# The start of a fused attention and feed-forward kernel: queries computed tile by tile, x added on TensorE, conversions and transfers in another order

## The chip, the cores and the metric

The kernel runs on one core of a Trainium2 chip. The metric is device time in microseconds. The core has TensorE (the rows PE and, for its weight loads, PEld), VectorE (DVE), ScalarE (ACT), GpSimd (POOL) and SyncE (SP). Each works through its own list of instructions in order, and they wait for one another by semaphores. Transfers are issued by SP, POOL or ACT.

## The reference

Input: 4096 tokens of 256 features in fp32. One block of linear attention (no softmax), a layer norm, a gated feed-forward net of width 1024 and a second layer norm:

```python
Q, K, V = x @ wq.T, x @ wk.T, x @ wv.T            # 64 columns each
energy  = K.T @ V                                 # 64 x 64, over all tokens
x = layernorm(x + (Q @ energy * sqrt(3/64)) @ wo.T)
h = silu(x @ w1.T * s1) * (x @ w2.T * s2)         # 1024 wide
h = gelu(h @ h1.T * hs1)
h = gelu(h @ h2.T * hs2)
x = layernorm(x + h @ w3.T * s3)
```

The energy needs the keys and values of all tokens before the first token's attention can be finished. Nothing behind it can start before it.

## The kernel before

The tokens are cut into eight tiles of 512 (`T`), the tiles are numbered 0 to 7, and a tile has four blocks of 128 tokens (index `s`). TensorE's outputs go to eight PSUM banks of 128x512 fp32; `aux` is banks 6 and 7, `ring` the three pairs (4, 5), (0, 1) and (2, 3). Most products keep fp32 accuracy by cutting one operand in two: ACT casts it to the rounded format `fp32r` (`hi`), DVE subtracts to get the rest (`lo`), and TensorE multiplies both parts with weights that are exact in that format. Products of plain fp32 operands run as two matmul records each.

The kernel has a start, in which keys, values, queries and the energy are made, and then four passes over pairs of tiles: gates (16 steps, eight column groups for each of two tiles), two square layers of 1024x1024 done with sums and differences of quarter matrices, and the last product with its norm. The start overlaps with the first pass, and the change lies there. The order of every engine's instructions is the order of the Python code (a manual schedule); no planner moves them.

In order, the start does this:

- Transfers. SP issues the first tile `xt[0]` in two halves with the weights `wkv` between them (L440, L442), then tiles 1 to 7 (L444), with `wq` behind tile 3, then `raw_blocks(0, 0)`, a transfer of a square layer's raw weights (L471), the tokens `x` of tile 0 and the scales. POOL issues `wo`, and `w1` and `w2` in halves (L530, L534); each waits for an earlier transfer by `after`. The loads of `x` of tile 1 on SP wait until the first half of `w1` has landed; `raw_blocks(0, 1)`, `s3` and `raw_blocks(0, 2)` stand behind them on SP.
- Six warm-up products (L549), then `keys_values` of tiles 0 to 3 (L574), each evacuated by an ACT copy of the whole bank (L580).
- `halves` of tiles 4 and 5 (L624 `hi` on ACT, L625 `lo` on DVE), all emitted behind the copy of tile 3, then `with_queries` of tiles 4 to 7 (L593): keys, values and queries in one product, evacuated in two groups `g` (L598, L599 on ACT, L600 on DVE). `halves(t + 1)` goes ahead of `with_queries(t)`.
- `two_queries(0)` (L645): queries of tiles 0 and 1, one in the upper, one in the lower 64 partitions of a bank; `stack` (L653 on ACT, L655 on DVE) puts `hi` into one half of the partitions of `stk[t]` and `lo` into the other, so that one product with the stacked operand does both. Tiles 4 to 7 get theirs by a transposition on TensorE (`turn_queries`, L608) and an ACT copy (`put_queries`, L612).
- `energy` (L633, eight tiles into 64 columns of bank 6), scaled by ACT (`es`, L679), times `wo` (L682, bank 7), cut into `m2hi` (ACT, L683) and `m2lo` (DVE, L684).
- `attention_out(0)` (L140): four 256-column products for each of two groups, hi and lo, into banks 6 and 7. DVE adds them onto `x` (L163), takes statistics (L150, L152), adds the epsilon (L87); POOL raises to the power -1/2 (L88); DVE norms (L172). TensorE transposes the result (L203), ACT and DVE cut it (L211, L212): these are the operands of the gates.
- Between these stand products that fill TensorE: `two_queries(2)` (tiles 2 and 3) in two parts, `turn_queries` of tiles 4 to 7.
- The first three gate steps for the first 256 tokens (`first_products`, L728; ring pairs 0, 1, 2), with the transposition of the second 256 tokens behind step 1; then the same three steps for the second half (L718); then `attention_out(1)`, and `gate` for steps 0 to 2 (ACT's silu L737 and DVE's product L738 free the banks). From step 3 on all steps are 512 columns wide.
- `early[0]` to `early[3]` are sums of raw weight blocks on DVE (L310) with a store by POOL (L494); the first two need `raw_blocks(0, 0)`, the others `raw_blocks(0, 1)`.

Of the kernel before, what the change touches and what calls it, by code (L numbers as in the profile page):

```python
# [44 lines left out]
def block_kernel(ctx: ExitStack, tc: tile.TileContext, a: dict, out: bass.AP):  # L45
# [85 lines left out]

    def attention_out(t):
        ps = []
        for g in range(NS // 2):
            po = aux[g].rearrange("p (j e) -> p j e", j=2)

            for i, m in enumerate((m2hi, m2lo)):
                for j in range(2):
                    q = stk[t][:, (2 * g + j) * P : (2 * g + j + 1) * P]
                    nc.tensor.matmul(  # L140
                        po[:, j, :], q, m, start=(i == 0 and j == 0), stop=(i == 1 and j == 1),
                        skip_group_check=True,
                    )
            ps.append(po)
        return ps
# [7 lines left out]

    def attend_norm(t, x, ps, pool):

        mv = p2.tile([P, NS, 2], F32, tag="mv1", name=f"mv1_{t}")
        y = pool.tile([P, NS, E], F32, tag=f"x2_{t // 2 % 2}", name=f"x2_{t}", bufs=2)
        r = {}
        x2[t] = y

        def add(g, j=slice(0, 2)):
            u = x[:, 2 * g : 2 * g + 2, :][:, j, :]
            nc.vector.tensor_tensor(u, u, ps[g][:, j, :], ALU.add)  # L163

        def stats(g):
            norm_stats([x[:, 2 * g + j, :] for j in range(2)], mv, 2 * g)

        def root(g):
            r[g] = rstd_of(p2, mv[:, 2 * g : 2 * g + 2, :], "a", 2)

        def norm(s, engine=nc.vector):
            engine.tensor_scalar(  # L172
                y[:, s, :], x[:, s, :], mv[:, s, 0:1],
                r[s // 2][:, s % 2 : s % 2 + 1], ALU.subtract, ALU.mult,
            )

        def norm_on_act(minus):

            for s in range(NS):
                nc.scalar.activation(  # L180
                    y[:, s, :], x[:, s, :], AF.Identity, bias=minus[:, s : s + 1], scale=1.0
                )
                nc.scalar.activation(
                    y[:, s, :], y[:, s, :], AF.Identity, scale=r[s // 2][:, s % 2 : s % 2 + 1]
                )

        def minus_mean():
            m = p2.tile([P, NS], F32, tag="mm", name=f"mm{t}")
            nc.vector.tensor_scalar(m, mv[:, :, 0], -1.0, None, ALU.mult)
            return m  # L190

        norm.on_act = norm_on_act, minus_mean
        return add, stats, root, norm

    def turn_on_pe(t, slot):
# [4 lines left out]
        def turn(s0, s1):  # L200
            for k in range(KE):
                for s in range(s0, s1):
                    nc.tensor.transpose(  # L203
# [234 lines left out]
    last = {}  # L438
    for k in range(KE):
        nc.sync.dma_start(out=xt[0][:, k, :], in_=a["xt"][0][:, k, :])  # L440
        if k == 0:
            nc.sync.dma_start(out=wkv, in_=a["wkv"])  # L442
    for t in range(1, NT):
# [72 lines left out]
    for name, dst in (("s1", s1), ("s2", s2), ("hs1", hs1), ("hs2", hs2)):  # L516
        nc.sync.dma_start(out=dst, in_=a[name])


    def after(d, t):  # L520
# [14 lines left out]
    xs[1] = load_x(1, lambda d: after(d, "w1"))  # L535
    raw_blocks(0, 1, raws[1])
    nc.sync.dma_start(out=s3, in_=a["s3"].partition_broadcast(P))
    after(raw_blocks(0, 2, raws[2])[0], "w2")


    turn_of_acc = [7]

# [10 lines left out]

    pe = aux[0][:, :D]
    xh, xl, kv, pq = {}, {}, {}, {}
# [26 lines left out]
    def with_queries(t):  # L582
# [4 lines left out]
        for g in range(2):  # L587
            ps = acc()[:, : 2 * V].rearrange("p (s c) -> p s c", s=2)
            for j in range(2):
# [11 lines left out]
                q[:, c, 1, :], ps[:, :, 2 * D :], q[:, c, 0, :].bitcast(F32), ALU.subtract  # L601
            )

    def turn_queries(t):
        ps = acc()
        for s in range(NS):
# [11 lines left out]
    def halves(t):  # L618

        xh[t], xl[t] = places[t - WHOLE]  # L620
        n = 2 if t == WHOLE else 1
        for h in range(n):
# [14 lines left out]

    def two_queries(t, steps=range(4)):

        if t not in pq:  # L640
            pq[t] = pq[t + 1] = acc()
        for i in steps:
            c, k = slice((i // 2) * T // 2, (i // 2 + 1) * T // 2), i % 2
            for j in range(2):
                nc.tensor.matmul(  # L645
                    pq[t][j * D : (j + 1) * D, c], wq1[:, k, :], xt[t + j][:, k, c],
                    start=(k == 0), stop=(k == KE - 1),
                )

    def stack(t):  # L650

        up, down = (slice(0, D), slice(D, P))[:: 1 - 2 * (t % 2)]
        nc.scalar.copy(stk[t][up], pq[t][up])  # L653
        yield
        nc.vector.tensor_tensor(stk[t][down], pq[t][up], stk[t][up].bitcast(F32), ALU.subtract)  # L655
        yield

    early = [*sums(0, 0, raws[0]), *sums(0, 1, raws[1])]
    for t in range(NT):
        if t < WHOLE:  # L660
            keys_values(t)
            continue
        if t == WHOLE:
            halves(t)
            halves(t + 1)
        elif t + 1 < NT:
            halves(t + 1)
        with_queries(t)
    two_queries(0)
    early[0]()  # L670
    for _ in stack(0):
        pass
    stack1 = stack(1)
    next(stack1)

    for t in range(NT):
        energy(t)
    two_queries(2, [0])
    nc.scalar.mul(es, pe.unsqueeze(1).to_broadcast([P, 2, D]), CSCALE)  # L679
    early[1]()  # L680
    pm = aux[1][:, :E]
    nc.tensor.matmul(pm, es.rearrange("e c d -> e (c d)"), wo, start=True, stop=True)  # L682
    nc.scalar.copy(m2hi, pm)  # L683
    nc.vector.tensor_tensor(m2lo, pm, m2hi.bitcast(F32), ALU.subtract)  # L684
    next(stack1)
    turn_queries(WHOLE)
    po = attention_out(0)
    put_queries(WHOLE)
    for t in range(WHOLE + 1, NT):
        turn_queries(t)  # L690
        put_queries(t)
    two_queries(2, range(1, 4))
    add, stats, root, norm = attend_norm(0, xs[0], po, p2)
    for j in range(2):
        add(0, j)
    stats(0)
# [4 lines left out]
    norm(1)  # L701
    stats(1)
    root(1)
    slot = next_slot()
    turn, split = turn_on_pe(0, slot)
    turn(0, 2)
    split(0, 2)
    norm(2)
    norm(3)
    for t in (2, 3):  # L710
        for _ in stack(t):
            pass

# [28 lines left out]

    for o in range(3):
        first_products([*zip(ring[o], (w1, w2))], o, slot, slice(0, T // 2))
        if o == 1:
            turn(2, 4)
            split(2, 4)
            early[2]()
            early[3]()
    for o in range(3):  # L750
        for ps, w in zip(ring[o], (w1, w2)):
# [6 lines left out]
    nc.gpsimd.dma_start(out=w3, in_=a["w3"])  # L758
    gate(0, xb)
    gate(1, xb)  # L760
    add(0)
    gate(2, xb)
    add(1)
    for g in range(2):
        stats(g)
        root(g)
    turn, split = turn_on_pe(1, slot)
    for i in range(3, 2 * KH):
        for ps, w in zip(ring[i % 3], (w1, w2)):
            gate_products(ps, w, i % KH, slot, i // KH)  # L770
        gate(i, xb)
        if i == 3:
            for s in range(NS):
# [613 lines left out]
```

## Time and profile before

| | |
|---|---|
| Median of 3 runs | 641.39 us (639.77 to 643.33) |
| Profiled execution | 639.2 us, span 637.3 us |
| TensorE busy | 623.9 us, 98% |
| DVE busy | 487.8 us, 77% |
| ACT busy | 378.8 us, 59% |
| First matmul of keys and values | 3.80 us from the span's start |
| First matmul of tile 1 | 7.60 us |
| First `with_queries` | 14.42 us |
| First product of queries alone | 23.52 us |
| First gate product (L728) | 34.44 us |
| First 512-column gate product (step 3) | 43.10 us |
| First product of a square layer (L298) | 69.92 us |

All times inside an execution are counted from the start of the span. A line of the waits reads: engine and line that waited, what ended the wait, microseconds in total, number of waits, the longest. A matmul's row in the trace includes its way through the array, so that rows overlap; its cost to the next one is the distance from start to start.

### The profile page before, as it was taken

To read this page: it belongs to the slowest core of one execution; us is meant where nothing else is said; L and a number is where in the kernel's file an instruction comes from. 1 tells how busy PE (TensorE), PEld (TensorE's weight loads), DVE (VectorE), ACT (ScalarE), POOL (GpSimd) and SP (SyncE) were. 2 spreads that over 40 slices of the span, in tenths; PEclk is the share of its full clock that TensorE was granted. 3 is DMA by queue.
4 is the path that set the end of the run, shared out by engine and by line. 5 is a ranking of instruction groups with operands and counts; after the bars stand their busy time and mean duration, and the time that the engine had idled before them with its cause. 6 is when DMAs were issued, how large, how long until landed. Compare 5 with 4: busy or idle time off the path is not lost.

```text
span 637.3 us, 9037 instructions
## 1 busy us (share of the span) xinstructions
PE 623.9 (98%) x3173; PEld 527.1 (83%) x3173; DVE 487.8 (77%) x764; ACT 378.8 (59%) x542; POOL 218.0 (34%) x280
## 2 busy tenths in 40 slices
PE   7999999999999999999999999999999999999995
PEld 6878888888898888888898888888898888888895
DVE  1799984898678788888667798798676886697456
ACT  3545462659855374656755458757764557765574
POOL 1233113204865408405545604612653700000043
PEclk9999999999999999999999999999999999999998
DMA  8999769987652168647751135645861035543201
GB/s 322 289 361 301 239 212 361 271 278 227 168 162 70 49 220 267 218 145 217 227 152 34 66 117 187 227 163 174 227 164 32 35 125 176 168 161 132 100 1 68
DMA packets 59408, 113.31 MB, mean 178 GB/s; under 512 B 19776, under 2 KB 34112, under 8 KB 59232
## 3 DMA queue, kind: packets, MB, share of 16 engines
q1 hardware_dynamic: 41168, 74.28, 35.1%
q0 software_dynamic: 18192, 38.41, 19.8%
q8 instruction: 26, 0.43, 0.3%
q14 instruction: 22, 0.18, 0.1%
HBM read 96.94 MB, written 18.87 MB: 182 GB/s over the span
## 4 chain that ended last, share of the span: by engine, by line
PE 95%; DVE 2%; DMA 1%; ACT 1%; issue 1%; POOL 0%; SPq 0%; POOLq 0%; DVEq 0%
PE bank L298 64%; PE bank L718 18%; PE bank L873 9%; PE bank L140 1%; PE bank L574 1%; PE bank L593 1%; DMA f<-in_xt 1%; PE bank L645 0%; DVE stk L655 0%; DVE lo L625 0%; DVE bn L150 0%; PE bank L633 0%; ACT hi L624 0%; POOL ra L88 0%; PE bank L728 0%
## 5 line engine op out<-in xcount | busy, mean ns | idle before, releaser
L298 PE MATMUL bank<-hi,ws 128*128 128x512 f32 x896 | 348.7, 389 | 0.0
L298 PE MATMUL bank<-lo,ws 128*128 128x512 f32 x896 | 348.6, 389 | 0.0
L253 DVE TENSOR_TENSOR lo<-f,hi 128x1024 fp32r<-128x1024 f32 x142 | 168.3, 1224 | 59.6 <-ACT hi L252 59.0
L298 PEld LDWEIGHTS bank<-hi,ws 128*128 128x128 f32 x896 | 168.2, 188 | 34.9
L298 PEld LDWEIGHTS bank<-lo,ws 128*128 128x128 f32 x896 | 168.2, 188 | 34.9
L252 ACT CAST hi<-f 128x1024 fp32r<-128x1024 f32 x142 | 142.7, 1051 | 48.6 <-PE bank L298 25.1
L348 ACT ACTIVATE f<-f,hs 128x512 f32<-128x512 f32 x96 | 62.6, 715 | 68.7 <-DVE f L310 68.7
L718 PE MATMUL bank<-hi,w 128*128 128x512 f32 (+1 forms) x256 | 98.4, 386 | 0.0
L718 PE MATMUL bank<-lo,w 128*128 128x512 f32 (+1 forms) x256 | 98.1, 385 | 0.0
L737 ACT ACTIVATE f<-bank,s 128x512 f32<-128x512 f32 x64 | 44.0, 689 | 68.2 <-PE bank L718 63.7
L310 DVE TENSOR_TENSOR f<-f,f 128x1024 f32<-128x1024 f32 x64 | 76.5, 1221 | 4.5 <-ACT f L348 3.8
L310 DVE TENSOR_TENSOR f<-f,bank 128x512 f32<-128x512 f32 x96 | 61.4, 681 | 15.3 <-ACT f L403 11.3
L738 DVE SCALAR_TENSOR_TENSOR f<-bank,s,f 128x512 f32<-128x512 f32 x64 | 47.6, 748 | 25.1 <-PE bank L718 24.0
L873 PE MATMUL bank<-w,lo 128*128 128x256 f32 x240 | 57.9, 283 | 0.0
L873 PE MATMUL bank<-w,hi 128*128 128x256 f32 x240 | 57.9, 283 | 0.0
L237 POOL DMA_DIRECT2D xT<-x x96 | 52.2, 551 | 13.1 <-DMA stage<-in_h 5.5
L718 PEld LDWEIGHTS bank<-hi,w 128*128 128x128 f32 x256 | 48.1, 188 | 9.8 <-DVE d L882 0.4
L718 PEld LDWEIGHTS bank<-lo,w 128*128 128x128 f32 x256 | 48.1, 188 | 9.3
L835 POOL DMA_DIRECT2D stage<-in_h x16 | 9.2, 575 | 126.8 <-DVE stage L861 99.7
L873 PEld LDWEIGHTS bank<-w,lo 128*128 128x128 f32 x240 | 46.1, 192 | 0.2
L873 PEld LDWEIGHTS bank<-w,hi 128*128 128x128 f32 x240 | 46.0, 192 | 0.2
L403 ACT COPY f<-bank 128x512 f32<-128x512 f32 x32 | 18.6, 589 | 28.6 <-PE bank L298 28.5
(161 smaller groups left out, 545.2 us busy)
## 6 DMA issues: line engine op xcount, KB each, us to landing
ws<-sw SPq DMA_DIRECT2D x100, 512.0 KB, 3.5
sw<-so POOLq DMA_DIRECT2D x16, 512.0 KB, 4.9
stage<-in_h POOLq DMA_DIRECT2D x16, 512.0 KB, 5.0
ws<-in_h POOLq DMA_DIRECT2D x12, 512.0 KB, 6.4
sw<-in_h SPq DMA_DIRECT2D x12, 512.0 KB, 5.9
x<-in_x SPq DMA_DIRECT2D x16, 256.0 KB, 6.0
f<-in_xt SPq DMA_DIRECT2D x7, 512.0 KB, 7.3
f<-in_h SPq DMA_DIRECT2D x6, 512.0 KB, 9.8
```

The lines of the kernel that those rows point to most:

```text
L237: moves.popleft()()
L252: nc.scalar.copy(hi[:, c, :], src[:, c, :])
L253: nc.vector.tensor_tensor(lo[:, c, :], src[:, c, :], hi[:, c, :].bitcast(F32), ALU.subtract)
L298: nc.tensor.matmul(ps[2 * h + o], w[:, k, o * P : (o + 1) * P], part[i][:, k, :], start=start and k == 0 and i == 0, stop=k == HK - 1 and ...
L310: engine.tensor_tensor(dst, u, v, op)
L348: nc.scalar.activation(dst, src, AF.Gelu, scale=sc[:, o : o + 1])
L403: nc.scalar.copy(bb[:, o], al[o])
L718: nc.tensor.matmul(ps[:, c], w[:, k, o * P : (o + 1) * P], part[:, 2 * j + k, c], start=(k == 0 and i == 0), stop=(k == KE - 1 and i == 1),)
L737: nc.scalar.activation(g, pa, AF.Silu, scale=s1[:, o : o + 1])
L738: nc.vector.scalar_tensor_tensor(g, pb, s2[:, o : o + 1], g, ALU.mult, ALU.mult)
L835: nc.gpsimd.dma_start(out=st[:, :n], in_=src.rearrange("p k o -> p (k o)")[:, c : c + n])
L873: nc.tensor.matmul(ps[:, :E], part[q][:, k, s * P : (s + 1) * P], w3[:, k0 + k, :], start=i % 2 == 0 and k == 0 and q == 0, stop=i % 2 == ...
```

## The change

The change rearranges the start:

- Transfers. `wkv` and the second half of `xt[0]` are issued by ACT, the first half by SP. `raw_blocks(0, 1)` goes ahead of the loads of `x` of tile 1 on SP.
- Conversions. `halves(4)` is emitted between the keys and values of tiles 2 and 3, `halves(5)` behind tile 3; `halves(6)` and `halves(7)` go between and behind the two groups of `with_queries(4)`. Tile 7 is cut in two parts, as tile 4 is.
- Queries of tiles 0 to 3. `queries(t, ps)` computes one tile at a time, with its two halves of 256 tokens in the upper and lower 64 partitions, into half a bank. `stack(t)` becomes two casts and two subtractions of 64x256. Tile 0's queries stand ahead of the energy, tile 1's behind attention, tiles 2 and 3 between the first two gate steps, together with `turn_queries` of tiles 6 and 7.
- `x` of the first two blocks of tile 0 is added by TensorE: a product with the identity (`with_x`) begins the accumulation in bank 0, and the attention of group 0 goes on in that bank. Statistics and norms of these blocks read the bank; the DVE additions are gone. The second group is added by DVE as before.
- Banks: the energy and its product with `wo` go into bank 4, and fixed banks replace the turn of `acc()` for queries and turns.
- Gates: the first two steps, not three, are done in halves; step 2 is done in 512 columns, and the additions and statistics of tile 1 are interleaved accordingly. Transpositions run by block instead of by feature half. `early[2]` and `early[3]` change places with stacks and norms.

```diff
     def attend_norm(t, x, ps, pool, summed=()):
+        def total(s):
+            return ps[s // 2][:, s % 2, :] if s // 2 in summed else x[:, s, :]
...
+    nc.scalar.dma_start(out=wkv, in_=a["wkv"])
+    for k, queue in enumerate((nc.sync, nc.scalar)):
+        queue.dma_start(out=xt[0][:, k, :], in_=a["xt"][0][:, k, :])
...
+    raw_blocks(0, 1, raws[1])
...
-    turn_of_acc = [7]
+    turn_of_acc = [3]
...
-        n = 2 if t == WHOLE else 1
+        n = 2 if t in (WHOLE, NT - 1) else 1
...
+    def queries(t, ps):
+        pq[t] = ps
+        for k in range(KE):
+            for j in range(2):
+                nc.tensor.matmul(
+                    ps[j * D : (j + 1) * D], wq1[:, k, :],
+                    xt[t][:, k, j * T // 2 : (j + 1) * T // 2],
+                    start=(k == 0), stop=(k == KE - 1),
+                )
     def stack(t):
+        sides = [slice(j * D, (j + 1) * D) for j in range(2)]
+        halves = [stk[t][:, j * T // 2 : (j + 1) * T // 2] for j in range(2)]
+        for s, h in zip(sides, halves):
+            nc.scalar.copy(h[s], pq[t][s])
+        for s, o, h in zip(sides, sides[::-1], halves):
+            nc.vector.tensor_tensor(h[o], pq[t][s], h[s].bitcast(F32), ALU.subtract)
...
+    for t in range(3):
+        keys_values(t)
+    halves(4)
+    keys_values(3)
+    halves(5)
+    for t in range(WHOLE, NT):
+        for g, _ in enumerate(with_queries(t)):
+            if t == WHOLE:
+                halves(6 + g)
+    queries(0, bank[1][:, :E])
     early[0]()
+    stack(0)
     for t in range(NT):
         energy(t)
     nc.scalar.mul(es, pe.unsqueeze(1).to_broadcast([P, 2, D]), CSCALE)
     early[1]()
+    with_x(0)
     nc.tensor.matmul(pm, es.rearrange("e c d -> e (c d)"), wo, start=True, stop=True)
     nc.scalar.copy(m2hi, pm)
     nc.vector.tensor_tensor(m2lo, pm, m2hi.bitcast(F32), ALU.subtract)
+    with_x(1)
+    po = attention_out(0, (bank[0], aux[1]), (0,))
+    for t, ps in ((4, bank[5]), (5, bank[2])):
+        turn_queries(t, ps)
         put_queries(t)
+    queries(1, bank[1][:, E:])
+    add, stats, root, norm = attend_norm(0, xs[0], po, p2, (0,))
     stats(0)
     root(0)
     for j in range(2):
         add(1, j)
     norm(0)
     norm(1)
     turn(0, 2)
+    stack(1)
     split(0, 2)
+    stats(1)
+    root(1)
+    early[2]()
     norm(2)
     norm(3)
...
+    first_products([*zip(ring[0], (w1, w2))], 0, slot, slice(0, T // 2))
+    turn_queries(6, bank[3])
+    put_queries(6)
+    queries(2, bank[2][:, :E])
+    queries(3, bank[2][:, E:])
+    turn_queries(7, bank[3])
+    put_queries(7)
+    turn(2, 4)
+    split(2, 4)
+    first_products([*zip(ring[1], (w1, w2))], 1, slot, slice(0, T // 2))
+    early[3]()
+    stack(2)
+    stack(3)
+    for o in range(2):
         for ps, w in zip(ring[o], (w1, w2)):
             gate_products(ps, w, o, slot, 0, slice(T // 2, T))
...
     gate(0, xb)
+    add(0)
     gate(1, xb)
     add(1)
+    for i in range(2, 2 * KH):
...
+        if i == 2:
+            for g in range(2):
+                stats(g)
+                root(g)
```

## The prediction

> **What bounds the kernel now.** First the page: busy shares, and the chain that ended last.
>
> ```profile
> PE 623.9 (98%) x3173; PEld 527.1 (83%) x3173; DVE 487.8 (77%) x764; ACT 378.8 (59%) x542; POOL 218.0 (34%) x280
> ...
> PE   7999999999999999999999999999999999999995
> ...
> PE 95%; DVE 2%; DMA 1%; ACT 1%; issue 1%; POOL 0%; SPq 0%; POOLq 0%; DVEq 0%
> ```
>
> TensorE is the bound everywhere except in the first slices, and the diff touches only those. So the question is how many microseconds in which TensorE does nothing are left there. Second, TensorE's waits in the first 90 us:
>
> ```profile
> PE bank L574 <- DMA f<-in_xt: 1.3, 1, 1.3
> PE bank L593 <- ACT hi L624: 1.2, 1, 1.2
> PE bank L728 <- DVE stk L655: 0.9, 1, 0.9
> PE bank L593 <- DVE lo L625: 0.9, 2, 0.6
> PE bank L728 <- ACT hi L211: 0.2, 1, 0.2
> PE bank L203 <- DVE x L172: 0.2, 1, 0.2
> ```
>
> These add up to 4.7 us, but a matmul's modelled tail counts as busy, so I also compare stretches with pure work. Third, the busy time by stretch (columns: stretch, length, busy of PE, PEld, DVE, ACT, POOL, then the granted clock, DMA share, GB/s):
>
> ```profile
> 3.65:7.60 3.95, 2.54 (x17) 2.38 (x17) 0.43 (x2) 0.99 (x2) 0.00 (x0) 1.00 0.98 314
> 7.60:13.22 5.62, 5.62 (x48) 5.43 (x48) 0.53 (x3) 1.17 (x2) 0.00 (x0) 1.00 1.02 403
> 13.22:23.50 10.28, 8.21 (x65) 7.52 (x64) 6.54 (x12) 8.15 (x20) 4.17 (x6) 1.00 0.89 286
> 23.50:34.44 10.94, 10.46 (x127) 7.58 (x127) 8.83 (x24) 4.93 (x12) 2.27 (x3) 1.00 1.05 347
> 34.44:43.10 8.66, 7.72 (x60) 7.45 (x61) 7.72 (x17) 3.99 (x8) 2.70 (x4) 1.00 0.95 369
> 43.10:69.92 26.82, 26.82 (x131) 22.38 (x130) 26.15 (x47) 13.63 (x19) 9.77 (x15) 1.00 1.04 302
> 18.70:21.00 2.30, 1.69 (x16) 1.52 (x14) 1.93 (x4) 1.97 (x6) 1.99 (x3) 1.00 0.35 73
> ```
>
> From start-to-start times in the timeline, one record costs 0.117 us (keys and values, transposes), 0.112 (`with_queries`, and queries at 64 columns of the array), 0.029 (energy), 0.12 (256-column gate or attention) and 0.228 (512-column gate). Work and bubbles (time minus work) are then: tile 0 with the wait for tile 1, 1.9 and 2.1; tiles 4 to 7, 7.2 and 3.1; from the queries to the first gate product, 9.2 and 1.7; from there to gate step 3 at 43.10, 7.2 and 1.5. That is 8.4 us of bubbles, and none behind 43.10. DVE is busy 26.15 of the 26.82 us there: by the timeline it frees the banks for gate steps 13 and 14 only 0.1 us before TensorE wants them.
>
> **The change, part by part.** The clock row is 1.00 throughout, so times carry over.
>
> *First transfers.* Each issue on SP takes 0.38 to 0.43 us plus 0.05. `wkv` and the second half of tile 0 go to ACT's queue; that puts tile 1's issue at about 1.27 instead of 2.21. It landed 5.3 us after issue, at 7.55, bound by the bytes ahead of it; later tiles land every 1.3 to 1.45 us. With the same delay tile 1 lands at 6.6; with no effect, at 7.55. The second half of tile 0 landed at 5.04; ending it means 5.9 at the earliest, the lower bound for tile 1. I take 6.5, nearest to the issue rows. ACT loses 0.9 us to its two issues ahead of its table load, hidden before `wkv` lands. Tiles 1 to 3 then run from 6.5 to 12.1 (5.62 us). Bubble 2.1 becomes 1.0.
>
> *Conversions of tiles 4 to 7.* Before, `halves(4)` stood behind tile 3's copy on ACT, so TensorE waited from 13.22 to 14.42, and again at 19.79 for `lo` of tile 6. Now `halves(4)` goes ahead of that copy: ACT is free at 10.95 (tile 2's copy, 0.59), tile 4 has landed by then (11.7 minus 0.9), the casts take 0.62 each and `lo` 0.69 each, done by 12.8, so tile 4 starts without a gap. What is late next is tile 5: ACT does tile 3's copy to 12.75, `hi` (1.05) to 13.8, DVE's `lo` (1.23) to 15.05, while TensorE wants it at 14.1: a stall of 1.0. Behind it `halves(6)` and `halves(7)` (in two parts) follow tile 4's evacuations on ACT (0.37 + 0.27 each) and come in time, within 0.2. So 8.4 us instead of 10.28: queries start at 20.5 instead of 23.5.
>
> *From the queries to the first gate product.* Moved behind the first gate product: the queries of tiles 2 and 3 (1.8) and the turns of tiles 6 and 7 (0.94), 2.75 in all; those of tile 1 (0.9) go behind attention. Added: `x` by an identity, two full-width fp32 products. Nearest by shape is 0.234 per 256 columns and record (twice the 128-column row), 0.94 in all; the 64-column queries' 0.112 gives 0.45 as low end, the `wo` product's 0.35 mean gives 1.4 as high end. They stand in front of and behind the `wo` product, where TensorE waits for `es` and for `m2hi` and `m2lo`, so of 0.94 only 0.1 shows. If that cover goes, all of it does. Removed from DVE: two bank additions (0.75), and `stack(1)` (0.69) ahead of them. `bn_stats` now reads the bank: 0.37 each, as the SBUF row, since additions that read banks (0.375) cost no more; bounds 0.30 and 0.50.
>
> With 0 at the start of the queries: queries to 0.9, energy to 2.76, `es` to 3.15, `wo` product 3.25 to 3.95, `m2hi` to 4.35; DVE does the two sums and `stack(0)` (now two halves, 0.75) until 4.6, so `m2lo` ends at 5.0; attention's first group at 5.4; statistics 0.97 and the epsilon row 0.17 to 6.55; POOL's power 0.73 with 0.15 of handover to 7.43; two norms to 8.2; transposes to 8.6; `hi` 0.37; first gate product at 9.0. Fillers (turns of 4 and 5, one tile's queries, attention's second group) end at 7.55. Before, this took 10.94; work is 7.4, so the bubble is 1.6. The first gate product comes at 29.5 instead of 34.44. Its banks are free by then (bank 4 by `m2lo` at 5.0, bank 5 by tile 4's evacuation at 6.9); bank 0, which the norms now hold, is free at 8.2 and wanted at 13.4. The stores of the sums take 0.77 of POOL each; those of the first two are issued by 5.4, ahead of the power at 6.7, and `early[2]` stores behind the second power. Transposing by token block instead of by half lets the first two go before the second norm ends; 0.2 at most, counted.
>
> The Trainium skill (VectorE: DVE Perf Modes, The perf-mode tier table) says that fp32 `tensor_scalar` runs at double rate from SBUF and at single rate once an operand is in PSUM; by its clock that would add an estimated 0.13 us to each of the two norms on this chain and the sum would be 638.7. The trace doesn't show that double rate: norms from SBUF take 0.36 start to start, bank additions 0.375.
>
> *From the first gate product to step 3.* Work is 9.8: two first halves and two second halves 3.84, step 2 in one 1.82, turns 0.94, queries 1.8, attention 0.95 and transposes 0.47. `first_products(0)` waits 0.15 for `lo`. The old 0.94 wait for bank 2 goes; in its place step 2 wants banks 2 and 3 at 9.0+8.2, and DVE reaches `stack(2)` and `stack(3)` only behind `split(2,4)` (ends 14.75) and a sum (1.37): 16.1 + 4 x 0.4 = 17.7. Queued behind that on DVE are gate 0 and the addition of tile 1. That costs 0.55, with 0.1 of handover 0.8 in all: step 3 at 29.5 + 10.6 = 40.1 instead of 43.10.
>
> *DVE behind that.* Gate 0 starts 1.9 us ahead of step 3 (before: 1.6), one gate and both additions still fit, and the end of gate 2 and both additions stands at +1.6, as before (+1.67). So the 0.1 us of slack at steps 13 and 14 stays; nothing is charged. Without it each 0.1 of DVE delay is 0.1 of time.
>
> *Raw blocks.* SP waited from 16.8 to 23.4 for `w1` with the transfers idle (73 GB/s, last line above). `raw_blocks(0,1)` (1.05 MB) now goes ahead of that wait, and fills the hole. Behind it in time are `w1` and `w2` on POOL's queue; their first halves landed at 23.4 and 27.15, and are wanted at 29.5. At 400 GB/s 1.05 MB is 2.6 us, so at worst 29.75; I charge nothing. `x1`, `s3` and the third raw block stay behind SP's wait, as before; the blocks' first sum moves from 38.98 to about 31.6 and finds them landed.
>
> **Sum.** Bubbles 1.0 + 1.2 + 1.6 + 0.8 = 4.6 against 8.4; work 0.94 more for `x`, 0.1 less for the undivided third step: 8.4 - 4.6 - 0.84 = 3.0 us. The profiled execution had 639.2 us (span 637.3): 636.2 there. The median shown is 641.39, 2.2 higher: 638.4. Half a per cent, what a measurement can tell here, is 3.2 us, so 3.0 stands just inside it, and the other case lies next to it.
>
> **Rivals.** (A) The transfers give nothing: bytes, not issues, bound tile 1, as the DMA share of 0.98 to 7.60 and 1.02 behind it speaks for; against it the 0.83 share that one microsecond (4 to 5) shows. Tile 1 stays at 7.55, tile 0's second half shares with tile 1. Then 1.0 of the gain goes: 639.4. The Trainium skill's rule (DMA: Bandwidth & Descriptors, Issuing engines are not separate DMA queues) speaks for this one: queues share the same engines, and a second issuer saves issue time alone. (B) DVE becomes the bound: an idle time of 1.5 us that I saw nothing against in steps 0 to 3, or bank reads at 0.5, comes out at steps 9 to 14, where 0.1 is left. 1.5 lost: 639.9. (C) Better: tile 5's stall and that of banks 2 and 3 don't appear (0.5 and 0.5, order on ACT and DVE kinder than I have it): 637.2, and 636.4 with tile 1 at 5.9. (D) Slower: the weights. 2.75 us of TensorE work was moved behind the first gate product; if `raw_blocks(0,1)` holds up `w2`, that product waits with nothing to fill it. It decides from a landing at 32.5. If `w2` came as late as these blocks did before (36.5), the time would be 4.0 above: 645.4. For it: slow stretches of 143 and 168 GB/s at 24 to 26. Against: the idle hole holds half of these bytes.
>
> **How the numbers follow.** Forecast 0.50 (own range 637.2 to 639.4), A 0.15, B 0.13, C 0.15, D 0.07. Low end: C's best, 636.4, less 0.6 for a median of executions that spread by 3.6; high end: A and B together, 641.0, plus 0.3; that is 635.8 to 641.3. Faster by over 0.5% (below 638.2): C, and just under half of the forecast's, 0.40. Slower (above 644.6): D's far part, 0.04, and an effect that no row shows, 0.04; 0.08. The rest 0.52.
>
> **What would show it.** Right: tile 1 starts near 6.5; no wait of `with_queries` for `hi`, one of 1 us for `lo` in tile 5; first gate product near 29.5, step 3 near 40.1, no wait for `stk` but one for bank 2 or 3 at step 2. Wrong: a wait of gate products for a weight transfer; DVE waits inside steps 9 to 14; `bn_stats` over 0.5.

## The result and the profile after

The changed kernel takes 637.96 us in the median (637.49 to 639.29), the kernel before 641.39 beside it: a ratio of 0.9945 (95% interval 0.9921 to 0.9968), 3.4 us. The profiled execution has 637.49 us with a span of 635.6, against 639.2 and 637.3: here the difference is only 1.7 us. Both numbers are needed. The 1.7 is what the two traces can explain; the rest comes from how far executions of one kernel lie apart, and is taken up under what stays open. Measured again beside the experiments, the changed kernel's ratio is 0.9971 (0.9956 to 0.9986).

The page after, the same three rows as shown of before:

```profile
PE 623.6 (98%) x3169; PEld 526.8 (83%) x3169; DVE 488.0 (77%) x767; ACT 379.1 (60%) x547; POOL 218.0 (34%) x280
...
PE   8999999999999999999999999999999999999995
...
PE 93%; DMA 3%; DVE 2%; issue 0%; ACT 0%; SPq 0%; POOL 0%; DVEq 0%; POOLq 0%
```

TensorE's waits after (engine and line, what ended the wait, total us, number, longest):

```profile
PE bank L724 <- DVE stk L663: 1.0, 1, 1.0
PE bank L581 <- DMA f<-in_xt: 0.9, 2, 0.5
...
PE bank L600 <- DVE lo L632: 0.7, 1, 0.7
PE bank L210 <- DVE x L179: 0.4, 1, 0.4
PE bank L734 <- ACT hi L218: 0.4, 1, 0.4
```

The wait for `hi` of tile 4 (1.2) is gone. Those for transfers fall from 1.3 to 0.9, and they are now for the two halves of tile 0 (landed at 4.03 and 5.67), no longer for tile 1 (landed at 5.97). `lo` costs 0.7, now in tile 5. One wait for `stk` is still there, of the same size as before, only at another place: gate step 2 waits for the stacks of tiles 2 and 3.

The busy time by stretch (length, busy PE, PEld, DVE, ACT, POOL, granted clock, DMA share, GB/s), cut at the start of tile 1, of `with_queries`, of the queries, of the first gate product, of step 2 and of the square layer (the first cut is 0.06 ahead of tile 1's first record):

```profile
6.65:11.98 5.33, 5.33 (x50) 5.33 (x50) 0.89 (x4) 2.67 (x5) 0.30 (x1) 1.00 1.04 405
11.98:20.42 8.44, 7.72 (x67) 7.35 (x66) 6.14 (x13) 7.03 (x20) 3.88 (x6) 1.00 1.05 375
20.42:29.94 9.52, 8.70 (x107) 6.29 (x107) 7.82 (x20) 4.16 (x12) 2.26 (x3) 1.00 1.17 393
29.94:39.80 9.86, 8.86 (x68) 7.42 (x68) 7.55 (x21) 4.22 (x11) 2.81 (x4) 1.00 0.98 355
39.80:68.21 28.41, 28.41 (x136) 23.86 (x137) 27.72 (x49) 14.72 (x21) 9.67 (x14) 1.00 0.92 274
```

| us from the span's start | before | forecast | after |
|---|---|---|---|
| tile 1 starts | 7.60 | 6.5 | 6.71 |
| queries start | 23.52 | 20.5 | 20.42 |
| first gate product | 34.44 | 29.5 | 29.94 |
| DVE's product of gate 0 starts | 41.51 | 38.2 | 39.78 |
| step 2 as a 512-column step starts | - | 38.3 | 39.80 |
| square layer starts | 69.76 | 66.8 | 68.21 |
| queries to square layer | 46.24 | 46.3 | 47.79 |

(The last two forecasts are the prediction's step 3 at 40.1 plus 26.66, the length of the rest in the trace before; step 2 is step 3 less its 1.82. In the trace before, the square layer's first product starts at 69.76; the table of before, which has 69.92, is 0.16 late there.) Up to the queries 3.1 us are gained; between the queries and the square layer 1.55 are given back, none of them forecast. From the square layer to the end the traces have 567.6 us before and 567.4 after.

### The profile page after: what moved, and what is told of

It is laid out like the page before. It is cut to its first block, busy times and chain, and to the rows that moved or that the text cites. A ratio compares the mean times of both kernels' runs of the same rounds, so it can differ in the third digit from the quotient of the medians.

```text
span 635.6 us, 9039 instructions
## 1 busy us (share of the span) xinstructions
PE 623.6 (98%) x3169; PEld 526.8 (83%) x3169; DVE 488.0 (77%) x767; ACT 379.1 (60%) x547; POOL 218.0 (34%) x280
## 4 chain that ended last, share of the span: by engine, by line
PE 93%; DMA 3%; DVE 2%; issue 0%; ACT 0%; SPq 0%; POOL 0%; DVEq 0%; POOLq 0%
PE bank L305 64%; PE bank L724 18%; PE bank L885 9%; DMA f<-in_h 2%; PE bank L140 1%; DMA f<-in_xt 1%; DVE so L317 1%; PE bank L210 0%; DVE stk L663 0%; DVE bn L150 0%; PE bank L650 0%; PE bank L734 0%; DVE d L894 0%; PE bank L615 0%; ACT hi L218 0%
## 5 line engine op out<-in xcount | busy, mean ns | idle before, releaser
L744 DVE SCALAR_TENSOR_TENSOR f<-bank,s,f 128x512 f32<-128x512 f32 x64 | 47.7, 747 | 24.9 <-PE bank L724 23.8
```

What stands on the lines that cost most here:

```text
L744: nc.vector.scalar_tensor_tensor(g, pb, s2[:, o : o + 1], g, ALU.mult, ALU.mult)
```

## Where 1.55 us went back: what DVE does ahead of gate 0

DVE after, each line a stretch of one kind of instruction (start, length, how many, and the idle time ahead of it with what ended it):

```profile
28.10 0.99 DVE L179 TENSOR_SCALAR x<-bank,mv,ra 128x256 f32<-128x256 f32 x2 [0.26 <-POOL ra L88]
...
35.24 0.76 DVE L219 TENSOR_TENSOR lo<-bank,hi 128x256 fp32r<-128x256 f32 x2 [0.92 <-ACT hi L218]
35.91 0.68 DVE L317 TENSOR_TENSOR so<-f 128x512 fp32r<-128x512 f32 x1
36.51 0.69 DVE L317 TENSOR_TENSOR so<-f,so 128x512 fp32r<-128x512 f32 x1
37.22 0.86 DVE L663 TENSOR_TENSOR stk<-bank,stk 64x256 fp32r<-64x256 f32 x2
38.89 0.86 DVE L663 TENSOR_TENSOR stk<-bank,stk 64x256 fp32r<-64x256 f32 x2 [0.81 <-ACT stk L661]
39.78 0.75 DVE L744 SCALAR_TENSOR_TENSOR f<-bank,s,f 128x512 f32<-128x512 f32 x1
```

and ACT beside it:

```profile
38.12 0.74 ACT L661 CAST stk<-bank 64x256 fp32r<-64x256 f32 x2 [2.00 <-DVE stk L663]
```

ACT's casts of `stack(3)` wait until DVE's subtractions of `stack(2)` are done, though they read and write other data; what the two have in common is bank 2, which holds the queries of both tiles in its halves. That it is the bank and not the tile `stk` is argued from the same trace: where casts and subtractions of `stk` read different banks they overlap (a subtraction of `with_queries` from 17.97 to 18.24, a cast from 18.12). So the two engines take turns, DVE stands idle for 0.81, and both gate 0 on DVE and step 2 on TensorE start only at 39.8. The trace before had nearly the same wait, with the queries of tiles 2 and 3 in the two partition halves of one bank, and the prediction did not use that row:

```profile
36.97 0.58 ACT L653 CAST stk<-bank 64x512 fp32r<-64x512 f32 x1 [1.84 <-DVE stk L655]
```

Two bounds then fix the square layer. From gate 0 on DVE works without a gap as far as gate 14, which starts 25.95 us later in after and 25.93 and 25.94 in the two kernels below it in the table; in no kernel here does the square layer come less than 28.2 us behind gate 0 (28.25 before); TensorE needs 28.4 us from a 512-column step 2, or 26.66 from step 3. The two lengths are read off these same traces. Each of the profiled executions below reaches the square layer at the later of the two:

| queries = 0 | gate 0 on DVE | step 2 in 512 columns | gate 0 + 28.2 | step 2 + 28.4 | square layer |
|---|---|---|---|---|---|
| before | 17.99 | (step 3 at 19.58) | 46.2 | (step 3 + 26.66) 46.2 | 46.24 |
| after | 19.36 | 19.38 | 47.6 | 47.8 | 47.79 |
| stacks cast first | 19.57 | 18.27 | 47.8 | 46.7 | 47.79 |
| one sum on POOL, nine warm-up products | 18.25 | 18.27 | 46.5 | 46.7 | 46.67 |
| `x` added by DVE | 19.74 | 19.77 | 47.9 | 48.2 | 48.16 |
| raw blocks late | 23.06 | 23.12 | 51.3 | 51.5 | 51.51 |

## The experiments

All times are medians; a ratio is to the kernel before beside it. Sessions differ: the unedited changed kernel has 637.96 in one and 639.35 in another, so a comparison with its 637.96 is good to 1.4 us, and the stretches of the traces decide where the medians can't. In the expectations, e3_stacks_first is "stacks cast first", e6 "all later sums on POOL" and e7 the changed kernel with nine warm-up products.

**The kernel before again**, unedited.

> The kernel before, once more, to see what differs between its executions. Its medians lie 3.4 us above the changed kernel's, its profiled execution only 1.7 (spans 637.3 and 635.6). Theory: part of the executions wait longer for a transfer; the nearest candidate is raw_blocks(0, 1), which landed at 36.5 us and whose sum on DVE started at 38.98, 2.5 us of margin, with DVE on the edge behind it. Then times spread over about 4 us (639.7 to 643.7), and a profile of a long execution shows DVE waiting for the transfer of raw blocks (f<-in_h) and the first product of a square layer 2 to 4 us after 69.92. Rival: the spread comes from somewhere else (weight loads of the square layers, the end), and the first 70 us are alike in every profile.

640.40 us (638.80 to 642.04), ratio 0.9992 (0.9975 to 1.0009). In its profile tile 1 starts at 8.81 instead of 7.60 and the queries at 24.73, but queries to square layer is 46.24 to the hundredth. Its DVE waits for no transfer from 20 to 72 us, so the theory doesn't show in this execution (640.61, not a long one); nor does the rival, since the first 70 us are not alike. Executions of one kernel differ ahead of the queries, and a stretch from the queries to the square layer repeats within 0.05 us.

**Raw blocks late.** `raw_blocks(0, 1)` goes back to its old place behind SP's wait for `w1`.

```diff
-    raw_blocks(0, 1, raws[1])
...
     xs[1] = load_x(1, lambda d: after(d, "w1"))
+    raw_blocks(0, 1, raws[1])
```

> The changed kernel with raw_blocks(0, 1) put back behind SP's wait for w1. Theory (the transfer matters): the blocks land near 35 us, the sum early[2] wants them at 32.25 us, DVE waits about 3 us for them, and with it the norms of the second half; the gain is gone or more than gone: 640 to 642 us, spread as wide as the kernel before. Rival (the move of the blocks hides nothing): time as the changed kernel, within 0.5 us, 638.

641.56 us (641.05 to 641.88), ratio 1.0018 (1.0002 to 1.0034): slower than after by 3.6 (2.2 by the repetition), and the whole gain is gone, as the theory had it. DVE's timeline shows why (`early[2]`, a sum of raw blocks, now stands ahead of norms that a gate step needs):

```profile
36.30 0.69 DVE L317 TENSOR_TENSOR so<-f 128x512 fp32r<-128x512 f32 x1 [4.04 <-DMA f<-in_h]
```

The prediction charged and credited this move with nothing. That was right as a number and says too little: together with the new place of `early[2]` the move is what keeps 3.7 us (51.51 against 47.79) from being lost.

**Stacks cast first.** Both casts of `stack(2)` and `stack(3)` go ahead of both subtractions, and all of it ahead of `early[3]`.

```diff
+    def stacks_apart(*ts):
...
+        for t in ts:
+            for s, h in zip(sides, halves[t]):
+                nc.scalar.copy(h[s], pq[t][s])
+        for t in ts:
+            for s, o, h in zip(sides, sides[::-1], halves[t]):
+                nc.vector.tensor_tensor(h[o], pq[t][s], h[s].bitcast(F32), ALU.subtract)
...
+    stacks_apart(2, 3)
     early[3]()
-    stack(2)
-    stack(3)
```

> The changed kernel with both tiles' casts of stack(2) and stack(3) ahead of both subtractions, and these ahead of early[3]. In the changed kernel ACT's cast for tile 3 waits for DVE's subtraction for tile 2 (2.0 us idle), and step 2 waits 1.0 us for it. Theory: that wait is an effect of the order of emission; without it banks 2 and 3 are free at about 37.7 us, step 2 starts at 38.65 instead of 39.80, and the whole gain of 1.1 us arrives: 636.9. Rival: DVE has no slack in the gate steps (0.1 us before the change), so that it comes back at steps 9 to 14 and the first product of a square layer stays at 68.2: 638.0.

638.49 us (637.84 to 640.09), ratio 0.9972 (0.9953 to 0.9992). TensorE's wait for `stk` is gone and step 2 starts 1.1 us sooner behind the queries (18.27), yet queries to square layer is 47.79 again. DVE's gate 0 stands at 19.57, and TensorE now waits for DVE later, inside the gates:

```profile
PE bank L210 <- DVE x L179: 0.6, 2, 0.4
```

(one of the two waits, 0.21, is at 48.28; after has only the other). The theory that the `stk` wait alone cost the microsecond fell; the rival, that DVE has no slack and a wait taken from TensorE comes back, held.

**One sum on POOL, nine warm-up products.** As the last, with `early[3]` given to POOL and `WARM` 9 instead of 6.

```diff
-WARM = 6
+WARM = 9
...
-    early = [*sums(0, 0, raws[0]), *sums(0, 1, raws[1])]
+    early = [*sums(0, 0, raws[0]), *sums(0, 1, raws[1], (nc.vector, nc.gpsimd))]
```

> e3_stacks_first with early[3] alone on POOL (its two sums, 1.30 us each there, fall beside DVE's work on banks; the later sums stay on DVE, where in e6 POOL's slowed DVE's 128x1024 subtractions from 1.2 to 2.1 us and their own from 1.30 to 2.1), and with nine warm-up products. Theory (DVE binds from m2lo to gate step 14): 1.37 us of DVE go, queries to square 46.7 to 46.9 instead of 47.79; with queries at 20.4 to 20.8 in every execution the time is 636.8 to 637.2, spread under 1 us, the lowest of all. Rival (TensorE's own gaps or POOL's share of the memory set the stretch): 47.8, and the time is e7's 637.9.

636.87 us (636.23 to 637.22), ratio 0.9933 (0.9916 to 0.9950). It is the lowest median here, 1.1 below after. It is also 1.0 below the changed kernel with the same nine warm-up products (637.88). Queries to square layer falls to 46.67, because DVE goes from the stacks straight to gate 0:

```profile
36.96 1.73 DVE L676 TENSOR_TENSOR stk<-bank,stk 64x256 fp32r<-64x256 f32 x4 [0.91 <-ACT stk L673]
38.73 0.75 DVE L757 SCALAR_TENSOR_TENSOR f<-bank,s,f 128x512 f32<-128x512 f32 x1
```

Against "stacks cast first", taking 1.37 us of sums off DVE ahead of gate 0 brings gate 0 forward by 1.32 and the square layer by 1.12; then TensorE is the bound again (step 2 + 28.4). With the stacks' order as it is here, that shows DVE's work ahead of gate 0 to be the cause of 1.1 us of the loss. The sum on POOL without the new order of the stacks was not run.

**All later sums on POOL.** As "stacks cast first", with `early[3]` and four sums inside the gate steps on POOL.

```diff
-                later = sums(0, i // 3, raws[i // 3])
+                later = sums(0, i // 3, raws[i // 3], (nc.gpsimd, nc.gpsimd))
```

> The kernel of e3_stacks_first with early[3] and the four later sums of raw blocks on POOL instead of DVE (POOL takes about 1.27 us for 128x512, by its row of 2.53 for 128x1024; DVE 0.69). Theory (DVE is the bound from the energy to gate step 14, so that e3's earlier step 2 came to nothing): 6.9 us of DVE work go, queries to square falls from 47.79 to about 46.7, and the time is 1.1 us below the changed kernel's. Rival (something else sets these 47.79 us, or POOL's work slows DVE's): 47.6 to 48.5, no gain.

640.00 us (638.14 to 640.93), ratio 0.9988 (0.9977 to 0.9999). Gate 0 comes as early as in the last kernel (18.25), but the square layer comes 30.1 behind it instead of 28.4, and 48.36 behind the queries, as the rival had it. DVE, then POOL:

```profile
48.52 4.19 DVE L260 TENSOR_TENSOR lo<-f,hi 128x1024 fp32r<-128x1024 f32 x2
```

```profile
49.74 1.88 POOL L317 TENSOR_TENSOR so<-xT 128x512 fp32r<-128x512 f32 x1
51.70 2.13 POOL L317 TENSOR_TENSOR so<-so,xT 128x512 fp32r<-128x512 f32 x1
...
61.08 1.30 POOL L317 TENSOR_TENSOR so<-so,f 128x512 fp32r<-128x512 f32 x1
```

The pair of DVE instructions took 2.34 in after; POOL's, run elsewhere, 1.30. Side by side both grow.

**First transfers on SP**, in the order of before.

```diff
-    nc.scalar.dma_start(out=wkv, in_=a["wkv"])
-    for k, queue in enumerate((nc.sync, nc.scalar)):
-        queue.dma_start(out=xt[0][:, k, :], in_=a["xt"][0][:, k, :])
+    for k in range(KE):
+        nc.sync.dma_start(out=xt[0][:, k, :], in_=a["xt"][0][:, k, :])
+        if k == 0:
+            nc.sync.dma_start(out=wkv, in_=a["wkv"])
```

> The changed kernel with the first transfers as before: xt[0] in two halves and wkv all on SP. Theory (the issue time counts): tile 1 starts at 7.6 instead of 6.65 us, all behind it is 0.9 later, 638.9. Rival (bytes bound the start; what is late at the issue is caught up in the conversions of tiles 4 to 7, which ACT paces): within 0.3 us of the changed kernel, 638.0.

639.62 us (637.82 to 642.16), ratio 0.9994 (0.9976 to 1.0013). Tile 1 starts at 8.50, later than expected, and the queries at 22.32, and TensorE waits for the tokens:

```profile
PE bank L582 <- DMA f<-in_xt: 2.2, 2, 1.6
```

Queries to square layer is 47.79 as in after. What the order of the issues does shows in the landings: with all first transfers on SP tile 1 lands at 7.55 to 8.84 us in four profiles (this one and three of the kernel before), with two of them on ACT at 5.97 to 6.54 in nine. How much of it reaches the queries depends on the start of the execution (last section): against the four profiles that were at full rate by 4.84, as this one was, it is 1.5 to 1.9 us; the four others, at half rate until 7.95 to 10.29, have their queries at 21.71 to 22.68 and lose most or all of it. In medians it is 1.7, or 0.3 against the repetition, and this kernel's own executions spread over 4.3 us; the theory's 638.9 and the rival's 638.0 both lie inside that.

**Conversions in the old order**, behind tile 3 and ahead of each `with_queries`, tile 7 in one part.

```diff
-        n = 2 if t in (WHOLE, NT - 1) else 1
+        n = 2 if t == WHOLE else 1
...
-    for t in range(3):
+    for t in range(WHOLE):
         keys_values(t)
     halves(4)
-    keys_values(3)
     halves(5)
     for t in range(WHOLE, NT):
-        for g, _ in enumerate(with_queries(t)):
-            if t == WHOLE:
-                halves(6 + g)
+        if WHOLE < t < NT - 1:
+            halves(t + 1)
+        for _ in with_queries(t):
+            pass
```

> The changed kernel with the conversions where they were: halves(4) and halves(5) behind tile 3's copy, halves(t + 1) ahead of with_queries(t), tile 7 in one part. Theory (ACT's order is what held TensorE up there): 1.2 us of waiting for hi come back and 0.6 for lo of tile 6 instead of the 0.7 for lo of tile 5, tile 1 to queries 15.9 instead of 13.8 us, time 2.1 above the changed kernel's. Rival (DVE binds behind it anyway): the loss is smaller than 1 us.

641.05 us (639.97 to 641.69), ratio 1.0004 (0.9990 to 1.0018). The waits of before are back:

```profile
PE bank L600 <- ACT hi L631: 1.2, 1, 1.2
...
PE bank L600 <- DVE lo L632: 0.9, 2, 0.6
```

These are 2.1 us of waits against 0.7 in after. From tile 1 to the queries it takes 15.9 us instead of 13.7, as expected: the order of the conversions alone carries 2.2 us. In medians, against 637.96 and the repetition's 639.35, it is 3.1 or 1.7.

**`x` added by DVE**, as before, in the same bank.

```diff
-    with_x(0)
...
-    with_x(1)
-    po = attention_out(0, (bank[0], aux[1]), (0,))
+    po = attention_out(0, (bank[0], aux[1]))
...
-    add, stats, root, norm = attend_norm(0, xs[0], po, p2, (0,))
+    add, stats, root, norm = attend_norm(0, xs[0], po, p2)
+    for j in range(2):
+        add(0, j)
```

> The changed kernel without x on TensorE: no product with the identity, DVE adds x for the first group as before, and statistics and norms read SBUF. Theory (DVE binds): DVE has 0.75 us more for two additions and 0.26 less for two norms, TensorE's 0.94 of work goes from a place where it waited anyway; first gate product 0.4 to 0.5 later behind the queries (9.9 to 10.0 instead of 9.52), queries to square 48.2 to 48.4 instead of 47.79, time 0.5 above the changed kernel's. Rival (TensorE's added work is what the stretch pays): 47.0 to 47.3, faster.

638.92 us (637.66 to 640.54), ratio 0.9957 (0.9941 to 0.9973). The medians can't tell it from after. The stretch can: the first gate product comes at queries + 9.91 instead of 9.52, the square layer at 48.16 instead of 47.79. That is the theory's picture; the identity product is worth 0.37 us.

**The changed kernel again**, unedited.

> The changed kernel once more, beside the others. Theory (from the queries to the first square product every execution takes the same 47.79 us, as three profiles of this form show; what varies is when the queries start, and that hangs on the first transfers and on when the first products of keys and values go over to full rate): queries to square again 47.79, tile 0 to queries anything from 16 to 18 us. Against the kernel before, which takes 46.24 in that stretch: 1.6 to 3.5 us faster. Rival: the 3.4 us between the two medians is a property of the kernels, and shows in every comparison.

639.35 us (637.87 to 639.60), ratio 0.9971 (0.9956 to 0.9986), in two clusters: three executions at 637.9 to 638.1, six at 638.8 to 639.6. The profiled one (638.78) has its queries at 21.71 and the square layer 47.80 behind that; the 1.29 by which its queries are later than in after is the whole difference of the two profiled executions (637.49). By the ratio the change is worth 1.9 us here. The 3.4 of the first comparison does not come back, so the rival is out.

**Nine warm-up products**, in the changed kernel and in the kernel before.

```diff
-WARM = 6
+WARM = 9
```

> The changed kernel with nine instead of six warm-up products, so that TensorE is busy until about 5.0 us instead of 3.65, past the landing of the first tile (4.1 to 4.7). Theory (the first products of keys and values run at 0.16 instead of 0.117 us a record after an idle time, which is what makes executions differ): full rate from the first tile on, queries at 20.5 to 21.5 in every execution, spread of times under 1.5 us, median 0.5 to 1.0 lower than the changed kernel's beside it. Rival (the transfers alone make the spread): median up by 0.4 to 0.8, since the first tile waits for the warm-up products, and the spread stays.

> The kernel before with nine warm-up products; tile 0 then starts at about 5.0 instead of 3.8, and still ends ahead of tile 1's landing (7.6). Theory (part of its executions are long because TensorE goes over to the full rate late, or falls back at an idle hole of the start; they are those with a mean granted clock of 0.991 to 0.994): the granted clock is 0.995 or more in nearly all executions, the times above 641.5 go, median 0.5 to 1.0 lower, 639.5 to 640. Rival (the holes of 1.3 to 1.6 us at tile 1 and of 1.2 at tile 4 bring it down again whatever came before): the spread of 638.5 to 644 stays.

Changed kernel: 637.88 us (637.67 to 638.23), ratio 0.9959 (0.9946 to 0.9972). Kernel before: 640.32 (639.83 to 641.55), ratio 0.9983 (0.9969 to 0.9996). Neither is much faster than the best executions with six, but the spread shrinks: 0.6 us in five executions (1.0 in the six of "one sum on POOL") against 1.7 to 1.8 in the changed kernel, 1.7 in twelve against 3.2 to 5.6 in the kernel before. There three of the twelve still have a mean granted clock of 0.994 and take 641.1 to 641.6 us; none is lower. In the changed kernel the theory held (queries at 20.76); in the kernel before it held for nine of twelve. Queries to square layer is 47.79 and 46.29, untouched. With both start-ups steadied so, the change is worth 2.4 us (640.32 against 637.88, in two sessions).

## Why the prediction was right, and where it was not

**The median** (638.4 forecast, 637.96 measured, 0.53% below before) came out within half a microsecond. But two errors of 1.3 and 1.7 us cancel in it, and that is luck. The forecast for the profiled execution was 636.2; it has 637.49. And the step from there to a median added 2.2, the distance between the profiled execution and the median of before; in the changed kernel that distance is 0.5.

**First transfers and conversions: right in size, and partly by luck.** Tile 1 at 6.71 (forecast 6.5), `with_queries` without a wait for `hi`, tile 5's stall for `lo` of 0.7 (1.0), queries at 20.42 (20.5). Rival A, that the transfers give nothing, is out: the groups of landings (7.55 to 8.84 on SP, 5.97 to 6.54 with ACT) don't overlap, and each pair is further apart than the 0.94 us by which tile 1 is issued sooner. But what holds tile 1 to 6.71 is not its landing at 5.97. It is the second half of tile 0, which landed at 5.67 (5.00 before) and whose eight products run until then. The prediction also took the clock row's 1.00 for full rate from the start; the profiled execution was at full rate from 3.77, the repetition's only from 7.95, and there tile 1 starts at 8.00 and the queries at 21.71. And a record of keys and values costs 0.112 us, not 0.117: tiles 1 to 3 take 5.27 instead of 5.62, which makes up for the later start.

**Queries to the first gate product: 0.5 short.** Forecast 9.0, measured 9.52. By the same steps: `m2lo` ends at 4.98 (5.0); statistics start at 5.58 (5.4); norms start at 7.68 (7.43) and end at 8.67 (8.2). Of the miss 0.22 is the norms that read the bank. DVE's groups, kept apart by form (busy us, mean ns of one, idle before):

```profile
L179 DVE TENSOR_SCALAR x<-x,mv,ra 128x256 f32<-128x256 f32 x6 | 2.2, 417 | 0.0
...
L179 DVE TENSOR_SCALAR x<-bank,mv,ra 128x256 f32<-128x256 f32 x2 | 1.0, 538 | 0.3 <-POOL ra L88 0.3
```

The prediction took the bank additions as the nearest row and costed these norms like those from SBUF; they take 121 ns more each. The rule that it set against that row (the Trainium skill, VectorE: DVE Perf Modes, The perf-mode tier table) gave 0.13 for each, and the trace agrees with the rule. `bn_stats` from the bank takes 424 ns against 414, inside the bounds. The identity products were sized about right: they save 0.37 net.

**Bank 2 and 3 stall at step 2: mis-sized, the step that failed.** Forecast: stacks done at queries + 17.7, a stall of 0.55 and 0.1 of handover. Measured: DVE's second `lo` ends at 15.58 instead of 14.75, for the 0.5 above and 0.3 more; then the two stacks, put down as four subtractions of 0.4 one behind the other, take 2.53 with 0.81 of idle time in them, and end at 19.33. Missing was the wait of ACT for DVE over one bank; the trace before has a row that shows one.

**"DVE behind that: nothing is charged": wrong.** It rested on gate 0 starting at 38.2, 17.7 behind the queries. It started 19.36 behind them, and the square layer came 1.5 later than forecast, which is the sentence's own condition ("without it each 0.1 of DVE delay is 0.1 of time"). Rival B named the right engine and about the right price (1.5); its place, steps 0 to 3, was right, though no wait shows at steps 9 to 14, where it was to come out. Its cause, an idle time in which nothing was seen to be against it, was in the end the two engines' turns on a bank. With the stacks reordered and 1.37 us of DVE's work taken away, 1.1 of the loss is gone (46.67); what is left is about the 0.5 by which the first gate product comes late.

**Raw blocks and weights: right.** The halves of `w1` and `w2` that the first gate step needs land at 23.8 and 25.8, wanted at 29.94; rival D did not occur. Rival C did not either (by its own terms, 0.5 and 0.5 off 638.4, it would be 637.4 and not 637.2, and 636.8 with tile 1 at 5.9).

**What stays open.** Executions of before, 79 of them beside the experiments, show a mean granted clock of 0.991 to 0.998, and their times go with it: medians of 643.5 at 0.991 (7 executions), 641.6 at 0.993 and 0.994 (23) and 640.2 at 0.997 (15). The 16 of the changed kernel all have 0.996 or more. That fits a difference of medians larger than that of the traces, but no execution below 0.997 of either kernel was profiled, so where the clock is lost there isn't shown. This mean does not see the half rate at the start that the last section shows.

## What to carry to other kernels

In a stage where two engines are both busy without a gap, find for each the first instruction of its gapless chain and its length; the end is the later of the two, and here work moved off the one gained nothing until the other's chain started sooner. Before halves of two tiles are put side by side in one PSUM bank, see whether two engines empty that bank: here they took turns by bank, as far as the traces show, and not by data. Don't carry the distance between one profiled execution and a median over to another kernel.

## What the runs showed of the hardware

**A wait of 3.5 us halves TensorE's clock for 3.4 us.** In "raw blocks late" TensorE stands still from 34.65 to 38.10. By stretch:

```profile
37.00:38.00 1.00, 0.00 (x0) 0.00 (x0) 0.97 (x3) 0.00 (x0) 0.00 (x0) 1.00 1.05 430
38.00:39.00 1.00, 0.90 (x5) 0.78 (x6) 0.36 (x2) 0.07 (x1) 0.80 (x1) 0.63 0.95 385
39.00:40.00 1.00, 1.00 (x7) 1.00 (x7) 0.66 (x2) 0.99 (x4) 0.00 (x0) 0.50 0.89 260
40.00:41.00 1.00, 1.00 (x6) 1.00 (x6) 1.00 (x3) 0.21 (x1) 0.00 (x0) 0.50 0.94 315
41.00:42.00 1.00, 1.00 (x8) 1.00 (x7) 0.95 (x3) 0.00 (x0) 0.41 (x1) 0.66 0.99 399
42.00:43.00 1.00, 1.00 (x11) 1.00 (x10) 0.19 (x2) 0.75 (x3) 0.91 (x2) 1.00 0.89 348
```

The third column from the end is the granted clock: 0.50 in the middle. A 256-column record goes from start to start in 0.21 us there and in 0.12 behind it, and the transposes from 38.26 on follow each other by 0.20 to 0.22 instead of 0.11. The Trainium skill (TensorE: Matmul & The Clock Gate, Part 1: The HAM clock gate) has the clock halved after about 3.4 us idle and full again after about 3.4 us busy; this trace agrees with both. One such stretch is worth 1.7 us of clock, or 0.003 of this span: the steps in which the mean clock of the executions of before falls (0.997, 0.994, 0.991). This execution, with one such stretch, has 0.994, the other profiled ones 0.996 to 0.998. So one or two such stretches would fit the executions of before; for those it is argued, not shown.

**At the start, records run at half rate while the clock row says 1.00.** First "stacks cast first", then after:

```profile
6.00:7.00 1.00, 1.00 (x7) 1.00 (x7) 0.00 (x0) 0.00 (x0) 0.00 (x0) 1.00 1.01 414
```

```profile
6.00:7.00 1.00, 1.00 (x11) 1.00 (x11) 0.00 (x0) 0.09 (x1) 0.00 (x0) 1.00 1.03 422
```

The counts include records that only reach into the stretch, so the 0.16 us a record of the expectations is too low. From start to start the records of 128 columns take 0.213 us up to 8.7 in the first kernel, the spacing of the 256-column records at 0.50 above, and 0.112 in after. The row's 1.00 is no measurement there: the trace's list of granted clocks begins with an entry to full rate, at 8.83 us in the first kernel and at 3.77 in after, and the row counts the time ahead of it as full. That entry goes with the queries. In the eight profiles with the changed order of transfers and conversions it stands at 3.77 to 4.84 in four, whose queries start at 20.42 to 20.82, and at 7.95 to 10.29 in the other four, whose queries start at 21.71 to 22.68. A hole between the warm-up products and tile 0 does not decide it alone: it is 1.04 us in "stacks cast first" and 1.09 in "raw blocks late", which was at full rate from 4.13. With nine warm-up products the entry stands at 3.80 and 4.84 in the changed kernel and at 6.26 in the kernel before, and the spread shrinks as told above. The Trainium skill, in the same section (TensorE: Matmul & The Clock Gate, Part 1: The HAM clock gate), calls the ramp dependent on the run; the spreads agree.

**DVE and POOL slowed each other where DVE read two operands in SBUF.** In "all later sums on POOL" DVE's `lo<-f,hi` reads two tiles in SBUF and the pair took 4.19 instead of 2.34. In "one sum on POOL" POOL's sums, 1.31 and 1.30, ran beside DVE instructions that read one operand from a bank, and both kept their times. The Trainium skill (SBUF — State Buffer, Who interferes with whom) says that a DVE instruction with two SBUF inputs contends with a GpSimd one that reads SBUF; the trace agrees.
